# Two Ifs in a row instead of If and Else, and another engine that paces GpSimd's indirect DMAs

## The chip, the core and the metric

The kernel runs on one core of one Trainium2 chip. The core has five engines, each with its own in-order instruction queue: TensorE (PE, matmuls; the loading of its stationary operand is shown as PEld), VectorE (DVE), ScalarE (ACT), GpSimd (POOL) and SyncE (SP). They tell each other of finished work through semaphores: an instruction may add to a counter when it ends, and an instruction of another engine may wait until that counter has reached a value. SP issues the ordinary DMAs; POOL issues the indirect ones, whose row addresses come from a list of indices. The metric is the device time of one execution in microseconds. Lower is better.

## What is computed

The input is `x` of shape [16, 256, 128], that is 4096 tokens of 128 numbers. Six sublayers follow each other, each with a layer norm ahead of it:

```python
x = x + 0.5 * ffn0(layernorm(x))     # 8 experts, top 2, SwiGLU, and one shared expert
x = x + attn0(layernorm(x))          # 16 heads of size 8, softmax(q1 k1) - lamb * softmax(q2 k2), then a norm
x = x + 0.5 * ffn0(layernorm(x))
x = x + 0.5 * ffn1(layernorm(x))     # 8 experts, top 2, GELU gate
x = x + attn1(layernorm(x))          # 16 heads of size 8, causal
x = x + 0.5 * ffn1(layernorm(x))
```

In the FFNs each token uses the two experts with the highest gate values, weighted by softmax probabilities. All data are float32.

## The kernel before

The tokens stay in the core's memory as eight blocks `xs[n]` of 512 tokens. The first FFN of the first two blocks (`FIRST = 2`) is computed densely over all experts. Every other FFN is sparse and runs by parts, `FFN_PARTS`: the class `Sparse` computes for a part of one or two blocks the gate, the two chosen experts and a slot for every token and choice. Its steps are these:

- `dispatch` normalises the blocks (`normalized`, `statistics`): VectorE computes mean and variance, and POOL raises the variance to the power -1/2. This is the instruction `rstd<-rstd,mhalf`. VectorE then makes `xn` of it. The slots go into the tile `idx`.
- `scatter` writes each token's row twice into a DRAM array `slots_x`, by 16 indirect DMAs of 128 rows for a part of two blocks.
- `load_tiles` and `compute` load tiles of 128 slots and the weights of their expert, and run the expert's two layers. The result goes to `slots_y` in DRAM.
- `combine` gathers each token's two result rows by 16 indirect DMAs into buffers `g`, and `add_to_x` on VectorE adds them to `x` with their weight.

Attention runs by sequences of 256 tokens (`Attention`). `unit` issues four score matmuls `q,k` of 32 rows each, `exponentials` runs ScalarE over them, and `sums` runs 16 matmuls `ex,vaug`, each writing 32 partitions of one bank. The copy of that bank into `avs` is its eviction.

**What sets the order.** Every step is a Python generator, and the planner `Tasks` picks at each point the step that can start first by its own clock model `Clocks`, with the tables of ranks at the top of the file. The order that comes out is fixed for PE, ACT, DVE and SP (`tc.manual_schedule(engines=ORDERED)`). POOL is not among them: the layer that builds the program sorts POOL's instructions itself, from their dependencies.

**The pace of indirect DMAs.** POOL's transfers are held to the planner's time by `transfers`. When it issues one, it asks the clock model for the last instruction that is to have ended 1.0 us before the planned start, `last_before(start - 1.0)`, and makes the DMA depend on it. So the DMA waits for that instruction's semaphore. Before the change the candidates are the last 100 instructions of TensorE, which `Timed.go` records.

**The two arms.** A bound on the attention scores is computed on the core from the weights. Where it holds, the scores need no shift by their maximum, and the program `program(False)` is used; otherwise `program(True)`, with more work. Both are built into the kernel, under `If` and `Else` on the register `is_bounded` (line 1921 to 1967). With these inputs the first one is executed: the trace has no instruction of the second.

Of the kernel before, what the change touches and what calls it, by code (L numbers as in the profile page):

```python
# [24 lines left out]
SYNC = mybir.DependencyInfo(mybir.DependencyClass.Sync, mybir.DependencyReason.DATA)  # L25
# [67 lines left out]
class Clocks:  # L93
# [8 lines left out]
    def __init__(self):  # L102
        self.free = {e: 0.0 for e in ("PE", "ACT", "DVE", "POOL", "SP")}
        self.wrote, self.read = {}, {}
        self.pending = {}
        self.table = None
        self.pe = []
        self.turn = 0.0
        self.bytes_free = 0.0
        self.warm, self.window, self.worked = False, 0, {}  # L110
        self.known = {}
# [17 lines left out]

    def last_before(self, time):  # L130

        return next((i for end, i in reversed(self.pe) if end <= time), None)

    def expect(self, ap, n=1):
        self.pending[self.keys(ap)[0]] = n
# [92 lines left out]
class Timed:  # L228
# [5 lines left out]
    def __getattr__(self, op):  # L234
        f = getattr(self.engine, op)

        def go(*args, **kw):
            r = f(*args, **kw)  # L238
            aps = [v for v in (*args, *kw.values()) if isinstance(v, bass.AP)]
            out = kw.get("out", aps[0])  # L240
            self.book(op, out, [v for v in aps if v is not out], args, kw)
            if self.name == "PE":
                self.clocks.pe = [*self.clocks.pe[-99:], (self.clocks.free["PE"], r)]
            return r

        return go
# [157 lines left out]
def kernel(ctx: ExitStack, tc: tile.TileContext, a: dict, out: bass.AP):  # L404
# [46 lines left out]
    clocks = Clocks()  # L451
# [689 lines left out]
    def transfers(todo, when=(), pool=None):  # L1141

        for i in range(0, len(todo), 2):
            two = todo[i : i + 2]
            reads = [r for _, rs in two for r in rs]
            _, taken = yield Ask("POOL", reads, take=[(pool, len(two))] if pool else [], when=when)
            for j, (issue, _) in enumerate(two):
                start = clocks.start("POOL", reads)  # L1150
                dma, ins, o = issue(taken[j] if pool else None)
                if clocks.last_before(start - 1.0) is not None:
                    tc.add_manual_dep(dma.ins, clocks.last_before(start - 1.0).ins.name, SYNC, reason="pace")
                clocks.book("POOL", 1.26, ins, [o], by="DMA", end=lambda s: s + 2.3 + LATE_ROWS, start=start, apart=True)

    b_turn = Buffers([()])
# [2 lines left out]
    class Sparse:  # L1159
# [153 lines left out]
        def scatter(self, xns):  # L1313
            def one(c, j):
                def issue(_):
                    row = xns[c // NCH][:, c % NCH, :]
                    s = bare.gpsimd.indirect_dma_start(  # L1317
                        out=self.sx[:, :],
                        out_offset=bass.IndirectOffsetOnAxis(ap=self.idx[:, j, c : c + 1], axis=0),
                        in_=row, in_offset=None,  # L1320
                    )
                    for t in self.scattered:
                        tc.declare_no_dep(s.ins, t.ins, reason="no slot twice")
                    self.scattered.append(s)
                    self.is_scattered.hit()
                    return s, [row, self.idx], self.sx

                return issue, (self.idx,)

            for i in range(len(xns)):  # L1330
                todo = [one(c, j) for c in range(i * NCH, (i + 1) * NCH) for j in range(2)]
                yield from transfers(todo, [(is_clear[self.slots], CLEAR)])
                b_xn.put(xns[i])
# [202 lines left out]
        def combine(self):  # L1536

            yield Ask("POOL", (self.sy,), when=[(self.stored, -(-self.ntile // 2)), (self.weighed, 1)])

            def one(c, j):  # L1540
                def issue(g):
                    s = bare.gpsimd.indirect_dma_start(  # L1542
                        out=g[:, :], out_offset=None, in_=self.sy[:, :],
                        in_offset=bass.IndirectOffsetOnAxis(ap=self.idx[:, j, c : c + 1], axis=0),
                    )
                    tasks.add(self.at("add"), self.add_to_x(c, j, g))
                    return s, [self.sy, self.idx], g

                return issue, (self.sy, self.idx)

            yield from transfers([one(c, j) for c in range(self.nch) for j in range(2)], pool=b_g)
# [23 lines left out]
    is_bounded = bare.values_load(bounded[0:1, 0:1], min_val=0, max_val=1)  # L1575
# [302 lines left out]
    def masks():  # L1878
        bare.vector.tensor_copy(ident_bf, ident)
        for dst, row, col in ((mask_ts, 1, -1), (mask_st, -1, 1)):  # L1880
            m32 = b_s.free[0][:, : 3 * P].rearrange("p (b t) -> p b t", b=3)
            bare.gpsimd.memset(m32, 0.0)
            for blk in (0, 2):
                bare.gpsimd.affine_select(
                    out=m32[:, blk, :], in_=m32[:, blk, :], pattern=[[col, P]],
                    compare_op=ALU.is_ge, fill=MASKED, base=0, channel_multiplier=row,
                )
            bare.vector.tensor_copy(dst, m32.rearrange("p b t -> p (b t)"))

    def attention_ends():  # L1890
        for layer in range(2):
            ended[layer] = [Count() for _ in range(NBLK)]
            for n in range(NBLK):
                ended[layer][n].at(BPB, done[n][3 * layer + 2].hit)

    def program(shifted):
        tasks.add(200, gather_weights(1, b1_1, b1_1))
        for n in range(1, FIRST):
            tasks.add(10 + n, dense(n, 10 + n))
        tasks.add(3, derived(1))  # L1900
        i = 0
        for layer in range(2):
            for which in range(2):
                last = layer == 1 and which == 1
                k = 2 * layer + which
                for slots, (r, blocks) in enumerate(zip(FFN_RANK[k], FFN_PARTS[k])):
                    Sparse(i, layer, which, blocks, slots, r, last).add()
                    i += 1
            for n in range(NBLK):
                r = ATT_RANK[layer][n]  # L1910
                tasks.add(r + ATT_STEP[layer]["attend"], attend(layer, n, r, shifted))
        tasks.run()

    MASKERS = ("DVE", "POOL")
    ended = {}
    clocks.pe = []
    saved = copy.deepcopy(clocks.__dict__)
    counts = [c for row in done for c in row] + [all_done, dense_done, *is_clear, *is_ready, *made.values()]
    counts = [(c, c.n, dict(c.then)) for c in counts]
    kept = [(p, list(p.free)) for p in (bank, b_wt, b_xg, b_xnT, dense_acc)]  # L1920
    with tc.If(is_bounded != 0) as chosen:
        with tc.manual_schedule(engines=ORDERED):
            attention_ends()
            program(False)
# [3 lines left out]
    for pool, free in kept:  # L1928
        pool.free = free
    del runs[1:]  # L1930
    with chosen.Else():


        b_ex.free = ex_tiles[:2]

        def strips(srcs, t):
            t = t.rearrange("p (i g j s) -> p i g j s", i=len(srcs), g=G, j=4)
            bare.gpsimd.memset(t, 0.0)
            for i, raw in enumerate(srcs):
                bare.gpsimd.tensor_copy(  # L1940
                    t[:, i, :, :, 0:D], raw.rearrange("c (j g d) -> c g j d", j=4, d=D)
                )
            return t.rearrange("c i g j s -> c i g (j s)")

        room = [t.rearrange("p j t -> p (j t)") for t in ex_tiles[2:]]
        n2, n1 = 2 * G * P, G * P
        wq_strips = [strips(wq[0], room[0][:, :n2]), strips(wq[1], room[1][:, :n1])]
        wk_strips = [strips(wk[0], room[0][:, n2 : 2 * n2]), strips(wk[1], room[1][:, n1 : 2 * n1])]
        rest = room[1][:, 2 * n1 :].rearrange("p (i f) -> p i f", f=2 * P)
        ones_row = rest[:, 2, :P].rearrange("p (j s) -> p j s", j=4)  # L1950
        bare.gpsimd.memset(ones_row, 0.0)
        bare.gpsimd.memset(ones_row[:, :, D : D + 1], 1.0)
        k_ones = rest[:, 3, 0:1]
        t = bank.free[0]
        bare.tensor.matmul(
            t[:, 0:1], lhsT=ones_row[0:1].rearrange("p j s -> p (j s)"), rhs=ones[0:1, 0:1],
            start=True, stop=True,
        )
        bare.vector.tensor_copy(k_ones, t[:, 0:1])
        masks()  # L1960
        mpad = [rest[:, i].rearrange("p (c j s) -> p c j s", c=NT, j=4) for i in range(2)]
        for t in mpad:
            bare.gpsimd.memset(t, 0.0)
        b_mpad = Buffers(mpad)
        with tc.manual_schedule(engines=ORDERED):
            attention_ends()
            program(True)
# [32 lines left out]
```

## Time and profile before

| | |
|---|---|
| timed runs | 1395.30, 1395.25 and 1385.06 us; median 1395.25 |
| the profiled execution's own time | 1379.28 us |
| its span, first to last instruction | 1377.6 us |
| mean granted clock of TensorE | 0.940 |
| POOL: indirect DMAs | 232 gathers of 983 ns, 240 scatters of 997 ns, 8 smaller ones |
| POOL: `rstd` | 64, 64.2 us together |
| ordinary DMA queue | 199.97 MB, 48.3% of 16 engines' span |
| indirect DMA queue | 30.97 MB, 6.8% |

The profile is a hardware trace of one execution. "Busy" is the time in which an engine works; the chain of work that ended last is followed back from the last instruction, at each step to what released it. A row of the timeline has its start, its duration, engine, line, operation, what it writes and reads, and in brackets the idle time of the engine ahead of it with the work that ended this idle time. Nearly all instructions are recorded by one helper, so they carry line 238 and are told apart by the names of their tiles. The indirect DMAs are at lines 1317 (scatter) and 1542 (gather). "issue" is time in which an engine waited for nothing that the profile shows.

### The profile page before, as it was taken

Reading aid. Unit: us, or ns where it says so; the run is one execution under the profiler, and the core shown is the slowest. Engines: PE = TensorE matmul, PEld = TensorE weight load, DVE = VectorE, ACT = ScalarE, POOL = GpSimd, SP = SyncE. Lnnn points to the kernel's source line nnn. Section 1 sums busy time; section 2 is a strip of 40 time slices with the busy share of each in tenths; the row PEclk is TensorE's granted clock in tenths of the full one; section 3 lists DMA queues with packets and bytes.
Section 4 is the critical chain, followed back from the end, with each engine's and each line's share of the span. In section 5 each row is a group of like instructions: output and inputs, shape, how many; then the busy total and the mean of one; then the engine's idle time right before and its main releaser. Section 6 shows DMA issues by size and latency. Waiting matters only on the chain.

```text
span 1377.6 us, 30138 instructions
## 1 busy us (share of the span) xinstructions
PE 1207.8 (88%) x9850; PEld 854.0 (62%) x9850; DVE 943.9 (69%) x3255; ACT 810.5 (59%) x2013; POOL 621.2 (45%) x631
## 2 busy tenths in 40 slices
PE   6699999898999999999969889888788999978857
PEld 4354754466566556545668756577676678767757
DVE  5488876558558857774668787867767865657635
ACT  3256757675777777667734376555456568655421
POOL 2015036502543261266072676645665464555353
PEclk9789999999899999999999999898899989998979
DMA  6927621347554135114778846546476266877884
GB/s 159 275 83 209 193 63 37 115 111 202 161 175 142 37 107 149 51 54 132 210 275 259 282 150 180 167 139 214 150 245 205 62 207 193 272 244 222 283 207 144
DMA packets 210577, 232.97 MB, mean 169 GB/s; under 512 B 34205, under 2 KB 154712, under 8 KB 210410
## 3 DMA queue, kind: packets, MB, share of 16 engines
q1 hardware_dynamic: 195050, 199.97, 48.3%
q0 software_dynamic: 15360, 30.97, 6.8%
q8 instruction: 80, 1.31, 0.4%
q14 instruction: 87, 0.71, 0.2%
HBM read 183.33 MB, written 53.30 MB: 172 GB/s over the span
## 4 chain that ended last, share of the span: by engine, by line
PE 72%; DVE 7%; issue 6%; DMA 5%; ACT 4%; SPq 2%; another core or an unknown queue 1%; POOL 1%; DVEq 0%; POOLq 0%; ACTq 0%
PE bank L238 72%; SPq L238 2%; DVE h L238 2%; DMA cwb<-slots_x 2%; DMA g<-slots_y,idx 1%; ACT ex L238 1%; ACT s L238 1%; DVE ex L238 1%; DVE x L238 1%; DMA cwb<-cwD 1%; DVE q L238 1%; POOL g L1542 1%; DMA slots_y<-y 1%; ACT L238 0%
## 5 line engine op out<-in xcount | busy, mean ns | idle before, releaser
L238 ACT ACTIVATE ex<-bank 128x512 f32<-128x512 f32 (+1 forms) x768 | 383.4, 581 | 102.7 <-PE bank L238 85.8
L1542 POOL DMA_INDIRECT g<-slots_y,idx x232 | 228.1, 983 | 230.4 <-PE bank L238 166.3
L1317 POOL DMA_INDIRECT slots_x<-xn,idx x240 | 239.4, 997 | 175.8 <-PE bank L238 98.8
L238 PE MATMUL bank<-q,k 32*128 32x512 f32 (+1 forms) x1536 | 260.2, 632 | 13.6 <-issue 5.6
L238 PE MATMUL bank<-xT,wt 128*128 128x128 f32 x1452 | 205.6, 287 | 16.0 <-issue 8.3
L238 PEld LDWEIGHTS bank<-xT,wt 128*128 128x128 f32 x1452 | 185.5, 200 | 36.8 <-issue 16.6
L238 PE MATMUL bank<-ex,vaug 128*32 128x256 f32 (+1 forms) x3072 | 186.7, 370 | 7.5 <-issue 3.4
L238 ACT ACTIVATE s<-bank,wt 128x128 f32<-128x128 f32 x472 | 140.4, 382 | 79.7 <-PE bank L238 64.7
L238 POOL TENSOR_TENSOR rstd<-rstd,mhalf 128x4 f32<-128x4 f32 (+1 forms) x64 | 64.2, 1004 | 270.5 <-DVE rstd L238 264.3
L238 PEld LDWEIGHTS bank<-q,k 32*128 32x128 f32 x1536 | 98.7, 191 | 84.4 <-issue 41.7
L238 PEld LDWEIGHTS bank<-ex,vaug 128*32 128x32 f32 x3072 | 93.9, 111 | 82.4 <-issue 18.1
L238 DVE SCALAR_TENSOR_TENSOR h<-bank,wt,s 128x128 f32<-128x128 f32 x363 | 107.7, 343 | 41.6 <-ACT s L238 19.4
L238 PE MATMUL bank<-wt,h 128*128 128x128 f32 x726 | 114.8, 291 | 12.3 <-DVE h L238 8.5
L238 PEld LDWEIGHTS bank<-wt,h 128*128 128x128 f32 x726 | 97.4, 199 | 38.0 <-DVE h L238 13.8
L238 PE MATMUL bank<-xT,rw 128*128 128x128 f32 x720 | 110.5, 293 | 5.7 <-issue 2.5
L238 ACT COPY xT<-bank 128x256 f32<-128x256 f32 (+1 forms) x177 | 61.3, 380 | 81.8 <-PE bank L238 73.3
L238 PEld LDWEIGHTS bank<-xT,rw 128*128 128x128 f32 x720 | 98.6, 206 | 12.2 <-issue 6.6
L238 DVE COPY oall<-bank 128x144 f32<-128x144 f32 x96 | 29.2, 305 | 111.6 <-PE bank L238 84.2
L238 ACT COPY avs<-bank 128x256 f32<-128x256 f32 x94 | 35.6, 379 | 118.2 <-PE bank L238 100.6
L238 DVE TENSOR_TENSOR y<-bank,wt 128x128 f32<-128x128 f32 x236 | 59.3, 284 | 64.0 <-PE bank L238 39.9
L238 DVE SCALAR_TENSOR_TENSOR x<-g,wgt,x 128x128 f32<-128x128 f32 x232 | 81.0, 356 | 29.2 <-DMA g<-slots_y,idx 24.3
L238 POOL TENSOR_TENSOR ex<-ex,causal 128x512 f32<-128x512 f32 x58 | 74.2, 1298 | 41.7 <-ACT ex L238 36.8
(202 smaller groups left out, 1865.6 us busy)
## 6 DMA issues: line engine op xcount, KB each, us to landing
wt<-wcat SPq DMA_DIRECT2D x127, 450.0 KB
rw<-wcat SPq DMA_DIRECT2D x64, 450.0 KB
wt<-wcat SPq DMA_DIRECT2D x109, 257.0 KB
slots_y<-y SPq DMA_DIRECT2D x161, 128.0 KB
rw<-wcat SPq DMA_DIRECT2D x52, 257.0 KB
cwb<-slots_x SPq DMA_DIRECT2D x44, 256.0 KB
xg<-slots_x SPq DMA_DIRECT2D x32, 256.0 KB
slots_x<-zero SPq DMA_DIRECT2D x15, 384.0 KB
```

Of the source, the lines that this page charges most:

```text
L238: r = f(*args, **kw)
L1317: s = bare.gpsimd.indirect_dma_start(out=self.sx[:, :], out_offset=bass.IndirectOffsetOnAxis(ap=self.idx[:, j, c : c + 1], axis=0), in_=ro ...
L1542: s = bare.gpsimd.indirect_dma_start(out=g[:, :], out_offset=None, in_=self.sy[:, :], in_offset=bass.IndirectOffsetOnAxis(ap=self.idx[:, j ...
```

## The change

Two things are changed.

First, the arms. `with tc.If(is_bounded != 0) as chosen` and `with chosen.Else()` become two Ifs with opposite conditions. Each semaphore is a counter that only grows. With If and Else, both arms start from the same value and count through the same range. With two Ifs the second arm counts on from where the first ended. An arm that is not executed is replaced by a short block in which each engine waits until its own semaphores have the value from before the arm, and adds what the arm would have added.

Second, the pace. The clock model keeps the last 150 instructions of ScalarE and of VectorE instead of 100 of TensorE, and `last_before` takes the one of the two engines whose instruction ends last ahead of the given time. The limit of 1.0 us stays.

```diff
-        self.pe = []
+        self.ends = {"ACT": [], "DVE": []}
...
     def last_before(self, time):
 
-        return next((i for end, i in reversed(self.pe) if end <= time), None)
+        last = [next(((end, i) for end, i in reversed(l) if end <= time), None) for l in self.ends.values()]
+        return max((e for e in last if e is not None), key=lambda e: e[0], default=(0.0, None))[1]
...
-            if self.name == "PE":
-                self.clocks.pe = [*self.clocks.pe[-99:], (self.clocks.free["PE"], r)]
+            if self.name in self.clocks.ends:
+                ends = self.clocks.ends[self.name]
+                ends.append((self.clocks.free[self.name], r))
+                del ends[:-150]
...
-                if clocks.last_before(start - 1.0) is not None:
-                    tc.add_manual_dep(dma.ins, clocks.last_before(start - 1.0).ins.name, SYNC, reason="pace")
+                ahead = clocks.last_before(start - 1.0)
+                if ahead is not None:
+                    tc.add_manual_dep(dma.ins, ahead.ins.name, SYNC, reason="pace")
...
-    clocks.pe = []
+    clocks.ends = {e: [] for e in clocks.ends}
...
-    with tc.If(is_bounded != 0) as chosen:
+    with tc.If(is_bounded != 0):
         with tc.manual_schedule(engines=ORDERED):
             attention_ends()
             program(False)
...
-    with chosen.Else():
+    with tc.If(is_bounded == 0):
```

## The prediction

> **What bounds the kernel now.** I read the page's first and fourth parts, then the waits of POOL (GpSimd), the view of the tile `rstd`, the chain in order of time, and stretches of the timeline. Busy shares and the chain first:
>
> ```profile
> span 1377.6 us, 30138 instructions
> PE 1207.8 (88%) x9850; PEld 854.0 (62%) x9850; DVE 943.9 (69%) x3255; ACT 810.5 (59%) x2013; POOL 621.2 (45%) x631
> PE 72%; DVE 7%; issue 6%; DMA 5%; ACT 4%; SPq 2%; another core or an unknown queue 1%; POOL 1%; DVEq 0%; POOLq 0%; ACTq 0%
> ```
>
> TensorE carries 72% of the chain. DMAs (5%) and POOL (1%) are in it only at a few places, but the change touches just those: every one of POOL's 480 indirect transfers, and what stands among them in its queue. What POOL waits for:
>
> ```profile
> POOL rstd L238 <- DVE rstd L238: 264.3, 34, 43.1
> POOL g L1542 <- PE bank L238: 166.3, 67, 33.7
> POOL slots_x L1317 <- PE bank L238: 98.8, 88, 29.2
> ```
>
> Columns: sum in us, times, longest. 155 transfers are put down to a matmul, 265 us of idle time: the pacing wait that is to be exchanged. That is an upper figure. A wait for several semaphores is given to the one that came last, and idle time of an engine used 45% of the span is mostly harmless. Who waits for the other thing in POOL's queue, the power that ends a layer norm's statistics:
>
> ```profile
> who waited for it (us, times):
>   POOL rstd L238: 264.3, 34
>   PEld bank L238: 13.5, 13
>   DVE xn L238: 7.9, 5
>   PE bank L238: 4.7, 3
> ```
>
> About 21 of its 64 instances have an idle TensorE or VectorE behind them. So POOL's order matters more than its load.
>
> **Part 1: fewer increments on TensorE.** In the built programs the executed arm has 5238 matmuls; 3406 tell a semaphore before the change and 2183 after. With both arms counting through the same values, an increment needed by one arm's wait was kept in the other, and POOL's pacing named matmuls (357 waits, 17 after). VectorE goes from 3057 to 2764 telling instructions, ScalarE from 1926 to 1907. No matmul, order or data transfer on PE, DVE, ACT or SP changes.
>
> What does an increment cost? First the row:
>
> ```profile
> 1366.97 4.63 PE L238 MATMUL bank<-y,s 128*128 128x128 f32 x40
> ```
>
> These are 20 fp32 matmuls, two records each. With 0.275 us for one record, 39 steps take 4.63 - 0.275 us, 112 ns each. Six of the 20 carry an increment, and steps after these are as long as the others. Over the whole trace the median step between 128x128 records is 112 ns with and without one; between instructions of ACT and DVE that do not wait it makes no difference either. The Trainium skill speaks otherwise: "TensorE: Matmul & The Clock Gate", section "The cost: per-tile semaphore tail", says that increments of packed matmuls are written one after another, 26.3 ns each. If each of the 1223 removed ones delayed TensorE by that, the change would save an estimated 32 us. The trace agrees only for the tail of a packed group: the eviction of `avs` starts 98 ns after the modelled end of its 16 packed `ex,vaug` matmuls where two of the last four tell, and 128 ns where three do (47 evictions). There the last four carry 209 increments in 96 groups, 97 after. So 112 x 30 ns = 3.4 us, if all were on the path. The view of waits has TensorE idle for `avs` 44 times in 96, and it has other work queued; I take a third, **-1.1 us** (bounds 0 and -32).
>
> **Part 2: the second If.** After its arm each engine now branches to the second comparison, jumps over the unused arm, waits for its own semaphore and adds to it. The present end:
>
> ```profile
> L1921 PEldq COMPARE_BRANCH  x2: 83/1777/3471, 67.7 to 1369.4; - x2
> L1921 DVEq COMPARE_BRANCH  x2: 51/53/55, 68.4 to 1371.7; - x2
> L1996 SPq EVENT_SEMAPHORE  x14: 17/28/28, 1375.9 to 1377.5; - x14
> L1996 DVEq DRAIN  x2: 10/34/57, 1374.7 to 1377.0; - x2
> ```
>
> The last store is issued at 1372.36 and SP goes on at 1375.9, so 3.5 us cover what the other engines do meanwhile. SP itself gets 9 more wait-and-add instructions; the present ones start 62 ns apart, 9 x 62 = 0.56 us. The far jump over the other arm exists already (DVE's drain starts 3.0 us after its branch); a further branch as slow as that would bring DVE to 1377.7 against the 1376.7 at which SP is ready, 1 us. The trace has no second branch: bounds 0.6 us (jump as short as the 0.05 us of its row) and 4 us (a 3.5 us jump, as PE's row, after the landing). I take **+1**, nearest to DVE's row, with its cover.
>
> **Part 3: new pace, new order on POOL.** The limit stays "1 us before the planned start"; only the engine whose last finished instruction is named changes. I looked up in the trace of before when each newly named ACT or DVE instruction ended. In 468 of 480 transfers that is ahead of the transfer's present start; in 12 it is later, by 7.7 us together. So as a pace it is nearly neutral. But POOL's order is not fixed by the kernel: the layer that builds the program sorts it, and it comes out differently. To price this I kept all other engines' rows and set each POOL instruction 0.28 us (the shortest delay in the trace) behind its named instruction or 0.28 us behind its predecessor. An example of a gain, two rows of which are in the chain (509.79 and 516.76):
>
> ```profile
> 509.79 1.02 POOL L238 TENSOR_TENSOR rstd<-rstd,mhalf 128x2 f32<-128x2 f32 x1 [0.56 <-DVE rstd L238]
> 511.00 1.01 POOL L1542 DMA_INDIRECT g<-slots_y,idx  x1 [0.19 <-issue]
> 515.53 1.03 POOL L238 TENSOR_TENSOR rstd<-rstd,mhalf 128x4 f32<-128x4 f32 x1 [3.52 <-DVE rstd L238]
> 516.76 1.01 POOL L1542 DMA_INDIRECT g<-slots_y,idx  x1 [0.19 <-issue]
> 518.07 0.96 POOL L1542 DMA_INDIRECT g<-slots_y,idx  x1 [0.30 <-PE bank L238]
> ```
>
> Here gathers stand blocked behind an `rstd` that waits for DVE. In the changed program four of them go ahead of it: the one of 516.76 starts about 2 us earlier, the `rstd` of 515.53 starts 1.4 us later. At 1081.55 the same exchange brings the gather 4.5 us forward and `rstd` of 1080.28 1.6 us back. The opposite:
>
> ```profile
> 421.25 0.95 POOL L1542 DMA_INDIRECT g<-slots_y,idx  x1 [0.30 <-issue]
> 422.22 1.04 POOL L238 TENSOR_TENSOR rstd<-rstd,mhalf 128x4 f32<-128x4 f32 x1
> 423.46 1.01 POOL L1542 DMA_INDIRECT g<-slots_y,idx  x1 [0.19 <-issue]
> ```
>
> Two gathers, 1.26 us each, now stand ahead of this `rstd`, which was ready: +2.5 us. And between 705 and 720, in the chain too, the gathers of 710.35 and 711.61 get behind later-released ones: they start near 716.4 and 718.9, and the batch ends 2.6 us later. VectorE adds the gathered rows in a fixed order, so behind such an add all of VectorE's queue stands, and TensorE's next in-order wait behind that.
>
> Sum on the chain: gains 2 + 4.5, halved because another input is late next: -3.2; losses 2.6 (at 716) and 0.9 + 1.6 (`rstd` at 509.79 and 1080.28): +5.1. Net +1.9. Off the chain 15 `rstd` move back by 24.1 us and 9 forward by 11.8; a third have somebody waiting, most with slack, so a tenth of the 12.3 counts: +1.2. Part 3 is **+3**.
>
> Total -1.1 + 1 + 3 = **+3 us**. The profiled execution, 1379.28 us (span 1377.6), would be 1382. It lies 16 us below the median of the timed runs, 1395.25 (two near 1395.3, one 1385.06); the same +3 on the median gives **1398 us**. With a spread of 0.7% between runs, about 1% is what a measurement here can tell from no change.
>
> **The rivals.**
>
> *Increments serialise everywhere* (faster). The skill's 26.3 ns on all 1223: 1395 - 32 + 4 = 1367. For it: the rule, and 36% fewer increments on the engine of the chain. Against it: equal steps of 112 ns in the rows. 6%.
>
> *Earlier gathers are worth their whole shift* (faster). Gathers start 0.4 us earlier on average, last ones of batches up to 5.5 us (917 and 1085). If sixteen batches each passed 1.5 us on, 24 us: 1374. Against it: DMA is 5% of the chain and `x` waits for `g` 24.3 us in all. 8%.
>
> *Layer norms late behind transfers* (slower). One mechanism: `rstd` ready, one to three transfers put ahead of it in POOL's queue. If all 26.6 us of late `rstd` reached TensorE and nothing of the gains, 1395 + 27 + 1 = 1423. It decides from about half of that, 14 us (1%). For it: 21 instances with a waiter; a stalled TensorE can lose clock too (the page shows slices at 0.7 and 0.8 of full clock). Against it: on the chain `rstd` has few pieces. 22%.
>
> *The change does not do what it says*: the built program shows it does; left out.
>
> **How the numbers follow.** Forecast, within 1% of before: 64%. Faster by over 1%: 6 + 8 = 14%; slower by over 1%: 22%. The forecast alone spans 1385 to 1409 (bounds of Parts 1 to 3 without the rule, and the runs' spread). For 8 in 10 the range takes most of either side, half of the slower rival's reach and half of the faster ones': 1377 to 1415.
>
> **What would show it.** Steps of 112 ns unchanged and PE's busy sum within 5 us: Part 1. `avs` starting some 70 ns after its matmuls: the tail. SP's last row 0.6 to 1.5 us longer after the store: Part 2. POOL's waits named ACT and DVE at similar sums, gathers ahead of `rstd` at about 515 and 1080, and waits of TensorE and DVE for `rstd` rising from 26 us to some 30 to 35: Part 3. The prediction is wrong if TensorE's own issue gaps shrink by tens of us, or the waits for `rstd` or `g` double.

## The result and the profile after

The changed kernel takes 1466.72 us (median of 4 runs, 1455.56 to 1474.09), the kernel before beside it 1394.18 us (4 runs). The ratio is 1.053, with a 95% interval of 1.045 to 1.061: **5% slower**, where 1398 us were forecast, in a range up to 1415. The profiled execution took 1455.56 us.

The page of the changed kernel, its first part and the chain:

```profile
span 1453.8 us, 30141 instructions
PE 1246.9 (86%) x9850; PEld 870.9 (60%) x9850; DVE 943.1 (65%) x3255; ACT 808.9 (56%) x2013; POOL 627.9 (43%) x631
PE 4%; another core or an unknown queue 2%; DMA 1%; ACT 1%; DVE 1%; issue 1%; POOL 0%; SPq 0%; ACTq 0%; DVEq 0%
```

The work is the same (DVE, ACT and POOL are busy as long as before within 7 us). TensorE is busy 39 us longer, at a mean granted clock of 0.917 instead of 0.940, and idle 37 us longer; the section on the prediction comes back to this clock. The chain breaks off after a tenth of the span, so it can't be read any further. What POOL (GpSimd) waits for, and who waits for `rstd`:

```profile
POOL rstd L239 <- DVE rstd L239: 248.8, 30, 40.3
POOL slots_x L1321 <- DVE idx L239: 59.3, 6, 28.3
POOL g L1546 <- issue: 50.5, 155, 1.3
POOL g L1546 <- ACT ex L239: 42.1, 14, 15.1
```

```profile
who waited for it (us, times):
  POOL rstd L239: 248.8, 30
  PEld bank L239: 11.0, 12
  POOL g L1546: 4.2, 3
  PE bank L239: 4.1, 2
  DVE xn L239: 3.1, 3
```

POOL's transfers no longer wait for TensorE. Over the whole view, waits of 175 of the 480 transfers are put down to ScalarE or VectorE (before: 21 to VectorE, 155 to TensorE), and 292 follow without any such wait ("issue"), against 285 before. So they stop about as often, but for other engines. TensorE and VectorE wait for `rstd` no longer than before, 18.2 us in the rows shown against 26.1. The end of the kernel, first the 20 fp32 matmuls, then SP's last rows:

```profile
1442.59 4.63 PE L239 MATMUL bank<-y,s 128*128 128x128 f32 x40
```

```profile
L1935 SPq EVENT_SEMAPHORE  x9: 17/17/17, 1451.5 to 1452.1; - x9
L2000 SPq EVENT_SEMAPHORE  x14: 17/28/28, 1452.2 to 1453.8; - x14
```

So matmul steps are unchanged, and the end after the last store (issued at 1447.98) is 5.8 us instead of 5.2. Neither explains the 76 us by which the profiled execution is longer. The view of waits of ScalarE gives the lead, here for the eviction `avs`, first before, then after:

```profile
ACT avs L238 <- PE bank L238: 100.6, 64, 8.6
ACT avs L238 <- remote: 7.1, 2, 4.8
```

```profile
ACT avs L239 <- PE bank L239: 74.3, 56, 5.6
ACT avs L239 <- remote: 55.4, 12, 10.6
```

"remote" stands for a wait whose end fits no instruction of the core that had just finished. Twelve evictions after the change end their wait so, against two before. One of them in the timeline of the changed kernel:

```profile
107.00 0.96 POOL L1321 DMA_INDIRECT slots_x<-xn,idx  x1 [0.30 <-issue]
107.19 1.93 PE L239 MATMUL bank<-ex,vaug 128*32 128x256 f32 x32
...
114.27 0.96 POOL L1321 DMA_INDIRECT slots_x<-xn,idx  x1 [0.30 <-issue]
...
118.07 0.96 POOL L1321 DMA_INDIRECT slots_x<-xn,idx  x1 [0.30 <-issue]
118.95 0.37 ACT L239 COPY avs<-bank 128x256 f32<-128x256 f32 x1 [10.64 <-remote]
119.38 0.69 PE L239 MATMUL bank<-ident,avs 128*128 128x128 f32 x2 [3.50 <-issue]
```

The 16 `ex,vaug` matmuls end at 109.12 by the profile, and TensorE has issued others since; the eviction that waits for them starts 9.83 us later. It is released while the last transfer of the series runs; the next one starts at 123.42. In the kernel before the same eviction was 3.37 us late:

```profile
111.79 1.93 PE L238 MATMUL bank<-ex,vaug 128*32 128x256 f32 x32
...
115.16 1.02 POOL L1317 DMA_INDIRECT slots_x<-xn,idx  x1 [0.30 <-issue]
...
117.10 0.37 ACT L238 COPY avs<-bank 128x256 f32<-128x256 f32 x1 [4.18 <-PE bank L238]
117.28 1.29 POOL L1317 DMA_INDIRECT slots_x<-xn,idx  x1 [1.10 <-PE bank L238]
```

To sum this up I took every instruction of ScalarE and VectorE that stood waiting for a matmul: its engine was idle from before the matmul's modelled end, and no other semaphore that it waits for came over 0.1 us after that end. Its delay is its start minus the matmul's modelled end (no view of the profile; worked out from the trace's rows, with the matmul that each waits for taken from the built program). Usually this is 0.04 to 0.11 us. Over 0.7 us I call it a *late release*. Before: 46 of 431, 84.7 us together, the longest 4.1. After: 60 of 460, 163.1 us, the longest 9.8. The sum is a measure of how much comes late, not of the loss: not every late release delays the end. ScalarE's waits for VectorE show nothing of the kind (0.03 us, with four such waits in each trace). So the question is what makes TensorE's completions come late, and which part of the change makes it worse.

### The profile page after: what moved, and what is told of

It is laid out like the page before. It is cut to its first block, busy times and chain, and to the rows that moved or that the text cites. A ratio compares the mean times of both kernels' runs of the same rounds, so it can differ in the third digit from the quotient of the medians.

```text
span 1453.8 us, 30141 instructions
## 1 busy us (share of the span) xinstructions
PE 1246.9 (86%) x9850; PEld 870.9 (60%) x9850; DVE 943.1 (65%) x3255; ACT 808.9 (56%) x2013; POOL 627.9 (43%) x631
## 5 line engine op out<-in xcount | busy, mean ns | idle before, releaser
L1546 POOL DMA_INDIRECT g<-slots_y,idx x232 | 232.0, 1000 | 235.7 <-issue 50.5
L239 PE MATMUL bank<-q,k 32*128 32x512 f32 (+1 forms) x1536 | 272.9, 640 | 12.1 <-issue 8.9
L239 PE MATMUL bank<-xT,wt 128*128 128x128 f32 x1452 | 214.9, 296 | 32.0 <-ACT xT L239 23.2
L239 PEld LDWEIGHTS bank<-xT,wt 128*128 128x128 f32 x1452 | 195.2, 209 | 53.9 <-ACT xT L239 27.9
L239 PE MATMUL bank<-ex,vaug 128*32 128x256 f32 (+1 forms) x3072 | 194.3, 381 | 11.0 <-ACT ex L239 5.1
L239 PE MATMUL bank<-wt,h 128*128 128x128 f32 x726 | 119.6, 297 | 19.0 <-DVE h L239 9.7
L239 PEld LDWEIGHTS bank<-wt,h 128*128 128x128 f32 x726 | 101.1, 205 | 46.7 <-issue 16.2
```

The costliest lines, as they stand in the source:

```text
L1546: s = bare.gpsimd.indirect_dma_start(out=g[:, :], out_offset=None, in_=self.sy[:, :], in_offset=bass.IndirectOffsetOnAxis(ap=self.idx[:, j ...
```

## The experiments

One observation first, without which no number can be read. Each kernel was measured together with the kernel before, on the same chip; such a group I call a set. In some sets the kernel before took 1386 to 1403 us (medians), as at first, and every version of the kernel profiled in them had at least 41 late releases; in others it took 1275 to 1280 us, and no version profiled in them had one (the longest delay was 0.5 us). I call them *held* and *free* sets. Two chips were met in both conditions, so it is not a property of the chip alone; what it is, I don't know. Each ratio is to the kernel before of the same set.

**Which part? (free set, before 1274.54).** My first theory was the increments: increments that nobody waits for are gathered into one when the program is built, so that the last of 16 `ex,vaug` matmuls tells 16 at once, and such evictions were among the late ones. `pace_only` keeps If and Else and takes the new pace; `ifs_only` does the opposite. `else_empty` and `each_told` change only the arm that isn't executed, which decides how many matmuls of the other one tell:

```diff
     with chosen.Else():
...
+        for i in range(5300):
+            bare.tensor.matmul(t[:, i % 64 : i % 64 + 1], lhsT=ident, rhs=ident[:, 0:1], start=True, stop=True)
+            bare.vector.tensor_copy(u[:, 0:1], t[:, i % 64 : i % 64 + 1])
```

> If and Else kept, only the pace is taken from ScalarE and VectorE. POOL's instructions stand as in the changed kernel; TensorE keeps 3287 telling matmuls (3406 before, 2183 in the changed kernel), and only 2 of its increments are 16 or larger (91 or so in the changed kernel). Theory A (the loss of 5% comes from increments that are gathered into one large addition on the last matmul of a group, which reach ScalarE late): within 1% of the kernel before, 1385 to 1405 us, and the view of waits has ACT idle for avs about as long as before (some 110 us). Theory B (the loss comes from the new pace and the new order on POOL): as slow as the changed kernel, 1455 to 1475 us.

> Two Ifs in a row, the pace still taken from TensorE. 2316 telling matmuls, 65 increments of 16 or more, because the pacing waits keep some in between. Theory A: most of the loss, in proportion 65 to 93 large additions some 50 us, 1430 to 1460 us. Theory B: as the kernel before plus the second comparison, 1393 to 1400 us.

> The kernel before with the arm of Else emptied to one instruction (the program for unbounded scores, which these inputs do not execute, is left out). The executed arm keeps its instructions, its pace on TensorE and its If and Else; only the increments that the other arm's waits had kept are gone: 2312 telling matmuls, 66 increments of 16 or more. Theory A: slower by as much as two Ifs alone, 1430 to 1460 us. Theory B, or a cost of the second comparison: 1393 to 1397 us.

> The kernel before with the arm of Else replaced by 5300 matmuls, each of which VectorE waits for (never executed; the program for unbounded scores is left out). So nothing in the executed arm changes but that 5237 of its 5238 matmuls tell, by 1 each, in place of 3406. Theory A: no gathered additions are left, so not slower than before, and up to 1% faster, 1375 to 1397 us. The rule that increments of packed matmuls are written one after another, 26.3 ns each: 1832 more of them, up to 48 us slower, 1443 us.

| kernel | telling matmuls | median us | ratio (95%) |
|---|---|---|---|
| `pace_only` | 3287 | 1268.38 | 0.996 (0.994 to 0.998) |
| `ifs_only` | 2316 | 1275.36 | 1.000 (0.997 to 1.002) |
| `else_empty` | 2312 | 1274.04 | 1.000 (0.997 to 1.003) |
| `each_told` | 5237 | 1272.47 | 1.000 (0.997 to 1.002) |

Nothing costs anything here, so no theory can be told from another. The same eviction in `pace_only`, with the changed kernel's stream of transfers, is 0.15 us after its matmuls:

```profile
108.12 1.93 PE L239 MATMUL bank<-ex,vaug 128*32 128x256 f32 x32
109.18 0.96 POOL L1321 DMA_INDIRECT slots_x<-xn,idx  x1 [0.30 <-DVE xn L239]
109.98 1.14 PE L239 MATMUL bank<-q,k 32*128 32x512 f32 x8
110.20 0.37 ACT L239 COPY avs<-bank 128x256 f32<-128x256 f32 x1 [0.96 <-PE bank L239]
```

**Increments or pace? (held set, before 1387.52).** The changed kernel again, and the changed kernel with If and Else, whose unused arm makes every matmul tell.

> The changed kernel once more, unaltered, beside the kernel before. In its profile ScalarE and VectorE waited 67 times for over 1 us longer than the recorded matmuls account for, in the kernel before 61 times; in the four kernels measured since, of which one has 2316 and one 5238 telling matmuls, not once, and all four took as long as the kernel before, 1268 to 1275 us. Theory C (the change costs only where the chip holds TensorE's completions back, and the chip did so when before and after were first compared): without such holds the changed kernel is within 1% of before, 1262 to 1287 us; with them, that is where the kernel before takes 1380 to 1400 us, 4 to 6% slower. Theory D (the two parts cost only together, whatever the chip does): 5% slower than the kernel before in any case, 1330 us where that takes 1274.

> The changed kernel's pace and order on POOL, but with If and Else, where the arm of Else is replaced by 5300 matmuls that VectorE waits for (the program for unbounded scores is left out). 5237 of the executed arm's 5238 matmuls tell, by 1 each, in place of 2183. Theory C: as the changed kernel where nothing is held back; where the chip holds completions back, faster than the changed kernel by over 2%, since no release hangs on an addition of 16. Theory D: as the kernel before, or as the pace alone, which took 0.996 of the kernel before.

Measured: 1451.62 us, ratio 1.046 (1.039 to 1.053), and 1457.26 us, 1.048 (1.039 to 1.057). Late releases 125.6 us (the longest 11.3) and 136.0 us (7.2). With 5237 single increments and no second If it is as slow as with 2183: the theory of gathered increments falls, and with it the second If as a cause. What the two kernels share is the pace and POOL's order. The traces also record TensorE's semaphore. Where its next increment came over 0.7 us after a telling matmul's end, POOL was issuing an indirect transfer in 61 to 63% of that time, against 33 to 35% of the whole span (the four traces of held sets so far). That gave theory E (what costs is that the transfers no longer wait for TensorE) and theory F (what costs is POOL's new order).

**Pace or order?** `new_order_old_pace` and `order_apart` are one kernel: two Ifs, TensorE's pace, and POOL's 601 instructions chained in the changed kernel's order. `old_order_new_pace` is its opposite.

```diff
+    at = {r.ins.name: r for r in ON_POOL}
+    order = [f"I-{n}" for n in POOL_ORDER]
+    for k, name in enumerate(order):
+        for ahead in order[max(k - 12, 0) : k]:
+            tc.add_manual_dep(at[name].ins, ahead, NOSYNC, reason="order")
     clocks.__dict__.update(saved)
```

> Two Ifs, the pace taken from TensorE as before (336 waits of POOL for it), but POOL's 601 instructions of the executed arm chained in exactly the order that they have in the changed kernel. Theory E (what costs is that POOL's transfers no longer wait for TensorE: while indirect transfers follow each other without a break, TensorE's completions are held back, and a transfer that itself waits for TensorE ends such a series): as the kernel before, within 1%, where that takes 1385 to 1400 us. Theory F (the new order on POOL costs): as the changed kernel, 4 to 5% slower, some 1450 us. Where the kernel before takes 1275 us, neither shows, and all are within 1%.

> The changed kernel, its pace on ScalarE and VectorE, with POOL's instructions chained in the order of the kernel before (12 of 601 still elsewhere). Theory E: 4 to 5% slower than before, some 1450 us where before takes 1387; the longest time for which completions are held back some 10 us against 5. Theory F: as the kernel before, within 1%.

> Two Ifs alone once more, pace on TensorE, for the case that the chip now holds completions back, which it did not when this kernel took 1.000 of before. Theories E and F alike: within 1% of before, since neither the pace nor the order is changed; the fewer telling matmuls (2316) and the second comparison cost nothing that can be measured. The theory of gathered additions (A), if it holds beside them: 2 to 4% slower.

This set was free (before 1276.85): 0.997 (0.995 to 0.999), 0.996 (0.994 to 0.999) and 0.997 (0.993 to 1.001). It told nothing apart, but shows once more that where nothing is held neither pace nor order costs anything. The old order with the new pace was not measured in a held set, so whether the new pace costs as much there stays open. The next set was held (before 1398.93):

> Two Ifs, the pace taken from TensorE, POOL's instructions in the order of the changed kernel: the kernel that was within 1% of before where before takes 1277 us, once more. Where the chip holds completions back (before at 1385 to 1400 us), theory E (POOL no longer waits for TensorE): within 1% of before. Theory F (the new order on POOL): 4 to 5% slower, some 1450 us. Where nothing is held back: within 1% again, and nothing is told apart.

Measured: 1399.36 us, ratio **0.999 (0.997 to 1.002)**, late releases 100.4 us, the longest 5.6. So the new order, two Ifs and 2303 telling matmuls cost nothing even where completions are held, as long as POOL waits for TensorE:

```profile
POOL g L1578 <- PE bank L271: 177.4, 63, 33.6
POOL slots_x L1353 <- PE bank L271: 70.6, 66, 6.8
```

F falls.

**Are the waits what matters?** `pace_on_all` is the changed kernel with the old waits put back beside the new ones; `last_pe_before` is the search of the kernel before, over TensorE's last 100 instructions.

```diff
                 if ahead is not None:
                     tc.add_manual_dep(dma.ins, ahead.ins.name, SYNC, reason="pace")
+                ahead = clocks.last_pe_before(start - 1.0)
+                if ahead is not None:
+                    tc.add_manual_dep(dma.ins, ahead.ins.name, SYNC, reason="pace")
```

> The changed kernel, whose indirect transfers wait for the latest instruction of ScalarE or VectorE and also, as before, for the latest matmul planned to end 1.0 us ahead: 351 waits of POOL for TensorE besides those for the other two. Theory E (a transfer that waits for TensorE ends the time in which completions are held back): within 1% of before, whether that takes 1275 or 1390 us. If the waits for ScalarE and VectorE cost by themselves: as the changed kernel, 4 to 5% slower where before takes 1390.

In a free set (before 1280.31) it took 1.005 (1.003 to 1.007). A second program has it together with the test of the next paragraph behind it:

> Two things one after the other in one program. First the changed kernel with the waits for TensorE put back beside those for ScalarE and VectorE (351 waits of POOL for TensorE), then the 24 phases of matmuls beside gathers (alone, row, paced, paced_late, evicted, spaced, four times each), which took 998 us by themselves and keep that length, since TensorE runs ahead of the evictions. Theory E, where the kernel before takes 1385 to 1400 us: the main program ends within 1% of before, at 1385 to 1410 us of the profile, not at 1440 to 1470; in the phases the releases of ScalarE are over 0.7 us late in row and paced_late, by up to several us, and never in alone, paced and evicted. If it is the rate of gathers that matters: late releases in row, paced and evicted alike, none in spaced. Where before takes 1275 us: the main program ends near 1285 us, and nothing is late.

This set was held (before 1402.78). The last store of the main program and the first matmul behind it:

```profile
1406.54 0.37 SPq L244 DMA_DIRECT2D out_dram<-x  x1
...
1409.91 2.90 PE L2017 MATMUL bank<-h,ident 128*128 128x512 f32 x3 [4.13 <-DVE h L1992]
```

In the changed kernel the span ends 5.8 us after this store's issue, and the time is 1.8 us longer than the span. That makes 1414.1 us for the main program in a run of 2438.56. That is 1.008 of before. The four runs' median is 2434.03; if the main program has all of the 4.5 us, it is 1409.6 us, 1.005 of before. This is an estimate without an interval, but the changed kernel's 4.6 to 5.3% would be 1467 to 1477 us. Late releases of the main program: 92.5 us, the longest 7.5. The order of POOL is not quite the changed kernel's here; with TensorE's waits, the two orders measured in held sets, the old and the new, took the same time. **With the waits for TensorE back, the loss is gone.**

**What holds completions?** `micro`, `micro_again` and `micro_pace` compute nothing of the reference: TensorE runs matmuls 128x512, ScalarE evicts them, and beside that other things happen.

> Another program, which computes nothing of the reference: input rows are copied to the output, and beside that TensorE runs groups of two 128x512 matmuls, each group evicted by ScalarE (24 groups, some 25 us, in a phase; every phase three times). In the phases POOL is idle, issues 16 gathers in a row, 16 scatters in a row, 16 additions of 512 columns, or SP issues 16 loads of 512 KB, or POOL issues 16 gathers of which each waits for a TensorE group two before. Theory E, where the chip holds completions back: ScalarE starts some 0.1 us after a group's end with POOL idle or adding, and up to several us after it in the phases of gathers and scatters in a row; the paced gathers in between. If the ordinary loads do it too, it is not the indirect transfers that matter. Where before takes 1275 us: 0.1 us in all phases.

> The program of matmul groups beside six kinds of work once more. Where nothing was held back, ScalarE started 0.09 us after each group's end in all six phases. Theory E, where the chip holds completions back: 0.1 us with POOL idle or adding, up to several us in the phases of gathers and scatters in a row.

> Nothing of the reference is computed. TensorE runs 48 single 128x512 matmuls in each phase (some 42 us), each evicted by ScalarE; POOL issues no gathers (alone), 16 in a row (row), 16 of which each waits for the matmul group 2 before the newest issued (paced), for the group 12 before (paced_late), for the eviction 2 before (evicted), or 16 with a 128x512 memset on POOL ahead of each (spaced). Each phase four times. Theory E, where completions are held back: holds of up to several us in row and paced_late, none over 0.7 us in paced and evicted, though the gathers follow at the same rate. If the rate of gathers alone matters: holds in paced as in row, none in spaced. Where before takes 1275 us: 0.09 us everywhere.

`micro` and `micro_pace` fell into free sets; the largest delay was 0.10 us. `micro_again` was held. ScalarE's delay is counted here from the matmul's end or from its own last instruction, whichever is later, so that the evictions that only queue up behind a late one don't count. Of the 72 evictions of each phase, those over 0.7 us late were: 6 beside gathers in a row (up to 3.0 us), 5 beside scatters in a row (up to 2.2), and none with POOL idle, adding, beside ordinary loads from SP's queue, or beside gathers that each wait for a matmul group. These last start every 1.72 us, against 1.26 in a row, so here the wait can't be told from the spacing. `all_and_micro` can do that; its phases of gathers, held too, have 192 evictions each:

| phase | gathers start every | over 0.7 us late | longest | phase takes |
|---|---|---|---|---|
| alone | none | 0 | 0.2 | 42.0 |
| row | 1.25 us | 15 | 2.9 | 44.6 to 46.3 |
| paced_late | 1.25 us | 15 | 3.0 | 46.4 to 47.1 |
| paced | 1.25 to 1.33, some 2 to 3.5 us | 12 | 1.9 | 42.0 |
| evicted | 1.25 to 1.33, some 2.7 to 4.1 us | 6 | 2.5 | 42.0 |
| spaced | 1.65 us | 0 | 0.4 | 42.0 |

(The very first phase, while the program starts, took 43.7 us.) The rows of "row", then of "paced", POOL and ScalarE:

```profile
1981.04 0.94 POOL L2003 DMA_INDIRECT g<-in_L_attn_x_dram,idx  x1 [0.30 <-issue]
...
1984.79 0.94 POOL L2003 DMA_INDIRECT g<-in_L_attn_x_dram,idx  x1 [0.31 <-issue]
1985.79 0.58 ACT L2022 COPY s<-bank 128x512 f32<-128x512 f32 x1 [2.93 <-PE bank L2017]
1986.04 0.94 POOL L2003 DMA_INDIRECT g<-in_L_attn_x_dram,idx  x1 [0.30 <-issue]
...
1988.59 0.58 ACT L2022 COPY s<-bank 128x512 f32<-128x512 f32 x1 [2.22 <-PE bank L2017]
```

```profile
1774.54 0.94 POOL L2003 DMA_INDIRECT g<-in_L_attn_x_dram,idx  x1 [0.30 <-issue]
1776.39 0.58 ACT L2022 COPY s<-bank 128x512 f32<-128x512 f32 x1 [2.07 <-PE bank L2017]
1777.80 2.54 ACT L2022 COPY s<-bank 128x512 f32<-128x512 f32 x5 [0.83 <-PE bank L2017]
1777.98 0.94 POOL L2003 DMA_INDIRECT g<-in_L_attn_x_dram,idx  x1 [2.50 <-PE bank L2017]
```

In "row" a completion is late and the gathers go on; the next ones are late too, and the phase gets 2.6 to 4.3 us longer. In "paced" the next gather waits for TensorE with everybody else. That leaves a gap of 2.50 us, and with it the hold is over; the phase is not longer. I had expected none over 0.7 us in "paced" and "evicted". That is a miss: 12 and 6 came late, and none with 1.65 us between the gathers, as the rival theory of the gathers' rate had said. So the wait doesn't prevent a hold, it ends it. A wait for a matmul long done ("paced_late") does nothing. A wait for an eviction ends holds as well, since the eviction itself waits for TensorE; in the changed kernel the named instruction of ScalarE or VectorE may be one that doesn't (that it was so is not shown).

The whole kernel agrees. I call the time from a telling matmul's end to the next recorded increment a hold, where it is over 0.7 us. Kernels with about as many telling matmuls can be compared. With TensorE's pace (`order_apart`) there were 154 holds, the longest 6.3 us, and at most 4 indirect transfers started in one; in the two held traces of the changed kernel there were 134 and 131, the longest 9.8 and 14.8 us, with up to 7 and 10 transfers. So without TensorE's waits holds were not more frequent, but the longest were longer.

**Can more be gained?** `spaced` puts a memset of some 0.5 us ahead of each transfer in the kernel before; `pe_pace_0` waits for a later matmul.

```diff
+                gap = bare.gpsimd.memset(pause, 0.0)
                 dma, ins, o = issue(taken[j] if pool else None)
```

```diff
-                if clocks.last_before(start - 1.0) is not None:
-                    tc.add_manual_dep(dma.ins, clocks.last_before(start - 1.0).ins.name, SYNC, reason="pace")
+                if clocks.last_before(start - 0.0) is not None:
+                    tc.add_manual_dep(dma.ins, clocks.last_before(start - 0.0).ins.name, SYNC, reason="pace")
```

> The kernel before with its pace on TensorE, POOL's instructions chained in the order they have there, and ahead of each of its 480 indirect transfers a memset of 128x512 bytes on POOL, some 0.4 us, which only spaces them; TensorE, ScalarE, VectorE and SP are unchanged. Theory E, where before takes 1385 to 1400 us: next to no completion is held back, and the kernel comes near the time it takes where nothing is held back, 1275 to 1330 us, 5 to 8% faster than before. If only waits on TensorE help: within 1% of before, or slower by what 480 x 0.4 = 192 us more work on POOL delays. Where before takes 1275 us: 0 to 2% slower, 1275 to 1300, since each batch of 16 transfers ends some 6 us later.

> The kernel before with one number changed: a transfer waits for the last matmul planned to end before its own planned start, not 1.0 us ahead of it. Theory E: where before takes 1390 us, a held-back completion stops the next transfer at once, so holds get shorter and the kernel is 1 to 3% faster, 1350 to 1385 us; transfers start some tenths of a us later, which nobody notices. Where before takes 1275 us: within 1%. If the length of the series doesn't matter: within 1% of before in either case.

> The kernel before with one number changed: a transfer waits for the last matmul planned to end before its own planned start, not 1.0 us ahead of it. Theory E, where before takes 1385 to 1400 us: holds end one transfer earlier, 1 to 3% faster, 1350 to 1385 us. If the length of the series doesn't matter further: within 1%. Where before takes 1275 us: 1.004 of it again.

`spaced` met a free set (before 1277.27) and took 1405.77 us, 1.100 (1.093 to 1.106). Nothing was held; the memsets made POOL slower, and VectorE waited 122.6 us for gathered rows, against 52.0 us in `each_told`:

```profile
L1181 POOL MEMSET pause<- 128x512 uint8 x480 | 259.7, 541 | 0.5
```

I had put 0 to 2% on that, counting the end of a batch only, not what stands behind it in POOL's queue (VectorE's waits for `rstd` are 51.8 us here). What it would do in a held set was not tried. `pe_pace_0` took 1.004 (1.000 to 1.008) in a free set (before 1280.31) and 0.999 (0.995 to 1.002) in a held one (before 1386.12; late releases 87.4 us). The expected gain of 1 to 3% isn't there. No version here is faster than the kernel before in a held set.

## Why the prediction was wrong

**The step that failed is in Part 3: "So as a pace it is nearly neutral."** It looked up when each newly named instruction had ended in the trace of before, and found it ahead of the transfer in 468 of 480 cases. So it priced the wait only by what it delays: POOL's start. The wait had another side, put at nothing without a reason: through it a late TensorE stopped POOL's transfers, and in the phases of matmuls a pause of the transfers ended the holds. The prediction called idle time such as the 265 us of POOL's waits for TensorE "mostly harmless"; some of these waits were of use. Where nothing is held, the step is right: 0.996 in a free set. In held sets, where the forecast was to be met, the missing waits cost 4.6 to 5.3%, 64 to 73 us: with the new order and TensorE's waits the loss was not there (0.999), with both kinds of wait hardly (1.005 by the estimate).

The sign was in the trace of before, and I passed over it. I looked for what transfers delay, not for what they disturb:

```profile
343.23 0.98 POOL L1542 DMA_INDIRECT g<-slots_y,idx  x1 [0.30 <-issue]
345.13 0.37 ACT L238 COPY avs<-bank 128x256 f32<-128x256 f32 x1 [4.78 <-remote]
345.54 0.95 POOL L1542 DMA_INDIRECT g<-slots_y,idx  x1 [1.33 <-remote]
```

The eviction and the paced transfer are released within 0.4 us of each other, 5.0 us after the end of the eviction's matmuls at 340.1. Somebody is late here, and both wait for it.

**Point by point.**

- *Part 1, increments cost next to nothing: right.* `each_told` has 1831 more than before and takes 1.000 of it; in a held set 5237 took as long as 2183. The rule of the Trainium skill ("TensorE: Matmul & The Clock Gate", "The cost: per-tile semaphore tail", 26.3 ns each) would make 48 us of the former, if it held everywhere. It holds for what its name says, the tail: the median start of `avs` after its packed matmuls was 67 ns with one of the last four telling (`ifs_only`), 93 ns in `pace_only`, 144 ns with all four (`each_told`), and 70 had been forecast. From one to four that is 26 ns each. Off the tail no run shows it. One sign named for this part did not come: TensorE's busy sum rose by 39 us instead of staying within 5, for the reason given under the clock.
- *Part 2, +1 us: right in size.* The end after the last store is 0.6 us longer (0.6 to 1.5 forecast); two Ifs alone are 1.000 and 0.997 of before, in free sets.
- *Part 3, new order, +3 us: small, as forecast.* With two Ifs and TensorE's waits, 0.999 in a held set (0.997 to 1.002, that is -4 to +3 us), which can't be told from nothing.
- *Rivals.* "Layer norms late behind transfers" was the slower case, with 1423 us, and isn't what happened: waits of TensorE and VectorE for `rstd` fell instead of rising to 30 to 35 us. "Earlier gathers" and "increments serialise" didn't happen either. What was missing is a rival in which the wait that is removed had been of use.
- *What would show it wrong.* Neither the issue gaps of TensorE shrank nor did the waits for `rstd` or `g` double, and yet it was wrong: these signs covered only the mechanisms thought of.
- *The clock.* A stalled TensorE was said to be able to lose clock. It did: 39 of the 76 us of the profiled execution are matmuls that take longer. The traces record the granted clock in steps of 3.4 us, at full or at half. It stood at half for 168 us before and 245 us after, and half of the difference is 38 us. In the hold of the kernel before shown above:

```profile
core 0: us, PE busy (x) PEld busy (x) DVE busy (x) ACT busy (x) POOL busy (x), PEclk, DMA share, GB/s
337.70:341.10 3.40, 3.40 (x42) 1.56 (x41) 1.95 (x7) 2.06 (x8) 1.77 (x3) 1.00 0.93 257
341.10:344.50 3.40, 0.71 (x8) 0.52 (x4) 0.98 (x4) 0.00 (x0) 2.50 (x3) 1.00 0.93 274
344.50:347.90 3.40, 2.34 (x10) 1.49 (x12) 1.75 (x9) 1.85 (x4) 1.91 (x2) 0.50 0.45 127
```

The clock falls in the step after the idle one. By the trace's clock records, from 80 us on it fell 26 times before and 39 times after; in 24 and 38 of these TensorE was busy for less than 80% of the step ahead, against 89 and 87% on average. The low clock is not what holds completions: `micro_again` had them held at a mean clock of 1.00, and `spaced`, where TensorE idles for another reason, ran at 0.92 to 0.93 with nothing held.

## What to carry to other kernels

Before exchanging a wait that looks harmless, ask what it stops when the engine that it waits for is late: a wait is also a brake, and its worth shows only when that engine is late. If GpSimd issues many indirect DMAs beside TensorE, let them wait for recent matmuls, not for instructions that go on without TensorE: here that was worth 4.6 to 5.3% in held sets and cost some 0.4% in free ones (`pace_only` and `old_order_new_pace`, 0.996 of before). When an engine's consumer starts long after the matmul's recorded end, compare what the other queues were doing in that gap.

## What the runs showed of the hardware

- With indirect gathers or scatters started by GpSimd every 1.25 to 1.27 us, ScalarE waited up to 3 us past a matmul's end in the small programs (`micro_again`, `all_and_micro`) and up to 11 us in the kernel (`both_parts`), in some sets of runs. With gathers every 1.65 us, beside ordinary loads, or beside GpSimd arithmetic it did not. Late completions were found of TensorE only.
- In held traces of the kernel 6 to 11% of the updates of TensorE's semaphore have no record of their own (before: 3099 for the 3464 telling matmuls of the whole program), in free ones under 1%. Whether they are merged or only not recorded isn't shown.
- The granted clock of TensorE fell to half mostly behind a step of 3.4 us in which TensorE was busy for less than 80% (38 of 39 times in the changed kernel, 24 of 26 before).
- The same kernel on the same chip took 1275 us in one set and 1399 in another. Late completions and the lower clock, 0.96 and 0.93, are the differences seen. Why completions are held, on which path, and what makes a set held, stays open. Every time on record comes with a recorded span and clock, so whether completions are held when nothing is recorded isn't known either.
